# Adjacency of a graph network: indirect DMA scatters, or products of one-hot matrices copied to SBUF strips

## The chip, the cores and the metric

The kernel runs on one core of a Trainium2 chip. TensorE (PE) multiplies matrices and writes to PSUM, VectorE (DVE), ScalarE (ACT) and GpSimd (POOL) work on rows of 128 partitions, and SyncE (SP) issues most transfers. The metric is the device time of one execution in microseconds. The time of the kernel before is the median of ten runs.

## The reference

A graph of 3125 nodes with 128 features and 50,000 weighted edges goes through four layers, each followed by a residual sum and a layer norm. The edges come sorted by their destination.

```python
edge_index = jnp.stack([src, dst])
x = _layernorm(x + L0(x, edge_index, edge_weight, ...))   # three graph convolutions with relu
x = _layernorm(x + L1(x, edge_index, ...))                # attention over the edges
x = _layernorm(x + L2(x, edge_index, edge_attr, ...))     # gated messages of the edges
x = _layernorm(x + L3(x, edge_index, edge_weight, ...))   # ten graph convolutions with layer norm and gelu
```

A graph convolution of layers 0 and 3 is, with a loop of weight 1 added at every node:

```python
deg = segment_sum(w, dst); dinv = rsqrt(deg); norm = dinv[src] * w * dinv[dst]
out = segment_sum((x @ W)[src] * norm[:, None], dst) + b
```

## The kernel before

The nodes are padded to 3200 rows, 25 tiles of 128 (`x`, laid out partition by tile), and the edges to 50,176, 392 columns of 128. A convolution is a dense product: the adjacency matrix, 3200 sources by 3125 destinations in f32, lies in DRAM in seven banks of 464 destination columns (the last has 341). `Convolutions.sums` multiplies one bank with the scaled features, 25 tiles into one PSUM tile `acc`; each f32 product is two passes on PE, so two matmuls in the profile. A bank is read in five pieces of five tiles (`adj_k`, 1160 KB); some pieces stay in SBUF for all layers (seven in layer 0, ten in layer 3). `acc` goes to `aggT`, is multiplied by the weights into `po` (line 685), and `done` adds bias and activation and writes the next layer's features `xs`. That second half of a bank is put into the next bank's products, after the seventh.

The matrix is made with scatters. In the front, `fill` (line 115) writes zeros and the identity to all banks, seven issues on ACT's queue. `SortedBuild` reads the edges in six passes, each with its neighbourhood: `compare` adds up edges with the same source and destination and computes addresses (`adj_index`, line 126), `split` and `degrees` build one-hot matrices of the destinations, which PE adds up to the degrees in `deg_ps`; `dinv` is their inverse root (line 536). `stretches` checks that the edges are sorted and that the assumptions of this path hold; its flag chooses between this path and a general one (lines 1611 to 1627). DVE runs all of it in an order written out by hand (`InOrder`).

After the branch `SortedBuild.scatter` (line 538) issues one indirect DMA for each of 406 columns of 128 edges, on POOL's queue. A load of a bank waits for the scatters of its pass (`after`, line 555). Since the scatters come bank by bank, the first two layers are computed in pieces in an order that a table `AHEAD` (line 38) gives: whatever is loaded is used at once, with partial sums kept in `part`. The third layer runs plainly. Banks run from the seventh down to the first.

`Attention` (line 1007) prepares tables for layer 1. Its constructor runs in the front: transfers through DRAM (`dst_pad`, then `wide`), `fresh`, `dl` and four PE transposes to `s_local`. `tables` (line 1081) writes each finished bank of layer 0 to the tables that layer 1 gathers from with POOL. Layers 1 and 2 are `l1_sorted` and `l2_sorted`, and `l3` runs ten convolutions.

Of the kernel before, what the change touches and what calls it, by code (L numbers as in the profile page):

```python
# [23 lines left out]
BW = 464  # L24
CK = 5
LATE = 6
SC = 14


PASSES = ((20, 28, 5, 7, 5), (16, 21, 0, 5, 4), (12, 16, 0, 4, 3), (8, 12, 0, 3, 2), (3, 8, 0, 2, 1),  # L30
          (0, 3, 0, 1, 0))
BELOW = ((20, 5), (16, 4), (12, 3), (8, 2), (3, 1))
FROM = ((21, 5),)
HALF = 5
ALL = (0, 1, 2, 3, 4)


AHEAD = ((0, 6, ALL), (0, 5, ALL), (0, 4, ALL), (1, 6, (0, 1)), (1, 5, (0, 1)), (1, 4, (0, 1)),
         (0, 3, ALL), (1, 3, (0, 1)),
         (0, 2, ALL), (1, 2, (0, 1, 2)), (1, 6, (2,)), (1, 5, (2,)), (1, 4, (2,)), (1, 3, (2,)),  # L40
         (0, 1, ALL), (1, 1, (0, 1, 2, 3)), (1, 6, (3,)), (1, 5, (3,)), (1, 4, (3,)), (1, 3, (3,)), (1, 2, (3,)),
         (0, 0, ALL), (1, 0, (0, 1, 2, 3)), (1, 6, (4,)), (1, 5, (4,)), (1, 4, (4,)), (1, 3, (4,)), (1, 2, (4,)),
         (1, 1, (4,)), (1, 0, (4,)))
# [3 lines left out]
SPAN = SC + 2 * NEAR  # L47
HEADS, HD = 4, 32
# [10 lines left out]
def tile_gnn_stack(ctx: ExitStack, tc: tile.TileContext, a: dict, out: bass.AP):  # L59
# [33 lines left out]
    tables_adj = [(dram.tile([SPARE + (b1 - b0) * NP * BW, 1], F32, name=f"adj{b0}"), b0, b1)  # L93
                  for b0, b1 in ((0, HALF), (HALF, NBK))]

    def bank(b):

        table, b0, _ = tables_adj[b >= HALF]
        at = SPARE + (b - b0) * NP * BW
        return table[at:at + NP * BW, :].rearrange("(t p c) o -> p t (c o)", p=P, c=BW)  # L100

# [13 lines left out]
    def fill(pool, banks):  # L115
        wide = NP - P + NBK * BW
        eye = pool.tile([P, wide], F32, name="eye")
        nc.vector.memset(eye[:, :NP - P], 0.0)
        nc.gpsimd.memset(eye[:, NP:], 0.0)
        nc.gpsimd.tensor_copy(eye[:, NP - P:NP], ident)  # L120
        for b in banks:
            v = eye[:, b * BW:b * BW + BW]
            nc.scalar.dma_start(bank(b), bass.AP(tensor=v.tensor, offset=v.offset,
                                                 ap=[v.ap[0], [P, NT], [1, BW]]))

    def adj_index(ve, at, hi_i, step, src, dst, table, lo, hi, outer):

        b0 = tables_adj[table][1]
        ve.tensor_single_scalar(hi_i, src, P.bit_length() - 1, op=OP.logical_shift_right)
        ve.scalar_tensor_tensor(at, hi_i, -2.0 * P, src, op0=OP.mult, op1=OP.add)  # L130
        ve.scalar_tensor_tensor(at, at, float(BW), dst, op0=OP.mult, op1=OP.add)
        ve.tensor_scalar_add(at, at, float(SPARE + (NP - P) * BW - b0 * BW + (lo - b0) * BW * (NP - 1)))
        for b in range(lo + 1, hi):
            ve.tensor_scalar(step, dst, b * BW - 0.5, float(BW * (NP - 1)), op0=OP.is_gt, op1=OP.mult)
            ve.tensor_add(at, at, step)
        ve.tensor_single_scalar(outer, dst, lo * BW - 0.5, op=OP.is_lt)
        ve.tensor_single_scalar(step, dst, hi * BW - 0.5, op=OP.is_gt)
        ve.tensor_max(outer, outer, step)
# [100 lines left out]
    def stretches(ve, between):  # L239
# [5 lines left out]
        with (  # L245
# [5 lines left out]
            nc.sync.dma_start(first_i[:, 1:NS], bass.AP(  # L251
                tensor=dst.tensor, offset=dst.offset + SE, ap=[[0, 1], [SE, NS - 1]]))
            ones = one.tile([P, P], F32, name="ones")
            nc.vector.memset(ones, 1.0)
            spread = one.tile([P, NS + 1], F32, name="spread")
            nc.vector.memset(spread, 0.0)
            nc.vector.tensor_copy(spread[0:1], first_i)
            firsts = ps.tile([P, NS + 1], F32, name="firsts")
            nc.tensor.matmul(firsts, ones, spread, start=True, stop=True)
            nc.vector.tensor_copy(first_f, firsts)  # L260
            run = one.tile([P, NCH + NEAR], I32, name="run")
            nc.vector.memset(run[:, NCH:], NP)
            nc.sync.dma_start(run[:, :NCH], bass.AP(
                tensor=dst.tensor, offset=dst.offset, ap=[[NCH, P], [1, NCH]]))
            nc.sync.dma_start(run[:P - 1, NCH:], bass.AP(
                tensor=dst.tensor, offset=dst.offset + NCH, ap=[[NCH, P - 1], [1, NEAR]]))
            between()
            bad = one.tile([P, 3 + len(BELOW + FROM)], F32, name="bad")
            for i, (c, b) in enumerate(BELOW + FROM):
                ve.tensor_single_scalar(bad[:, 3 + i:4 + i], first_f[:, c:c + 1], b * BW - 0.5,  # L270
                                               op=OP.is_gt if i < len(BELOW) else OP.is_lt)
            scr = one.tile([P, NCH], F32, name="scr")
            ve.scalar_tensor_tensor(scr, run[:, :NCH], 0.0, run[:, 1:NCH + 1], op0=OP.add,
                                           op1=OP.is_gt, accum_out=bad[:, 0:1])
            ve.tensor_tensor(scr, run[:, :NCH], run[:, NEAR:], op=OP.is_equal)
            ve.scalar_tensor_tensor(scr, run[:, :NCH], float(N), scr, op0=OP.is_lt, op1=OP.mult,
                                           accum_out=bad[:, 2:3])
            ve.scalar_tensor_tensor(scr[:, :NS], first_f[:, 1:], 1.0 - P, first_f[:, :NS],
                                           op0=OP.add, op1=OP.is_gt, accum_out=bad[:, 1:2])
            total = ps.tile([P, 3 + len(BELOW + FROM)], F32, name="total")  # L280
# [8 lines left out]
    def build():  # L289
        with (  # L290
# [4 lines left out]
        ):  # L295
            blank = b1.tile([P, NCH], F32, name="blank")
# [9 lines left out]
            for i, (table, t0, t1) in enumerate(tables_adj):  # L306
                nc.sync.dma_start(table[:SPARE, :].rearrange("(p c) o -> p (c o)", p=P), blank)
                place = b1.tile([P, NCH], F32, name=f"place{i}")
                outer = b1.tile([P, NCH], F32, name=f"outer{i}")
                step = b1.tile([P, NCH], F32, name="step")  # L310
                hi_i = b1.tile([P, NCH], I32, name="hi_of_src")
                adj_index(nc.vector, place, hi_i, step, cols.src_i, cols.dst_f, i, t0, t1, outer)
                away = first_rows(b1, 0, place, NCH, f"away{i}")
                places.append((table, place, outer, away))
# [66 lines left out]
    class SortedBuild:  # L381
# [5 lines left out]
        def __init__(self, pool):  # L387
            self.at, self.total, self.ready, self.last = [], [], {}, []
            self.passes = list(enumerate(PASSES))
            self.st = [self.load(pool, 0, nc.sync)]  # L390

        def load(self, pool, q, queue):

            W = NEAR - 1
            s0, s1, lo, hi, _ = PASSES[q]
            C, e0 = SC * (s1 - s0), SE * s0

            def window(v, name, left, none):
                t = pool.tile([P, left + C + W], v.dtype, name=f"{name}{q}")
                n = left + C + W  # L400

                def part(p0, p1, c0, c1):
                    queue.dma_start(t[p0:p1, c0:c1], bass.AP(
                        tensor=v.tensor, offset=v.offset + e0 + p0 * C - left + c0,
                        ap=[[C, p1 - p0], [1, c1 - c0]]))

                first, last = e0 < left, e0 + P * C + W > NCH * P
                assert not (first and last) and W <= C
                if first:
                    nc.vector.memset(t[:, :left], none)  # L410
                    part(0, P, left, n)
                    part(1, P, 0, left)
                elif last:
                    nc.vector.memset(t[:, left + C:], none)
                    part(0, P, 0, left + C)
                    part(0, P - 1, left + C, n)
                else:
                    part(0, P, 0, n)
                return t

            return {"C": C, "e0": e0, "banks": (lo, hi), "src": window(a["src_r"], "src_w", W, -1),
                    "dst": window(a["dst_r"], "dst_w", W, 0), "ew": window(a["ew_r"], "ew_w", 0, 0.0)}

        def prepare(self, pool, scratch, ps, ve):

            W, st = NEAR - 1, self.st
            st += [self.load(scratch, q, nc.gpsimd) for q in range(1, len(PASSES))]
            pe_ = InOrder(nc.tensor)
            iota_ps = ps.tile([P, P], F32, name="iota_b")
            deg_ps = ps.tile([P, 3, NT], F32, name="deg_ps")  # L430
            CM = SC * max(s1 - s0 for s0, s1, _, _, _ in PASSES)

            def neighbours(t, start, C):

                v = t[:, start:start + C]
                return bass.AP(tensor=v.tensor, offset=v.offset, ap=[v.ap[0], [1, C], [1, W]])

            def compare(q):

                t = st[q]  # L440
# [37 lines left out]
                at = pool.tile([P, C], I32, name=f"at{q}")  # L478
                ve.tensor_add(at, away, place)
                self.total.append(total)  # L480
                self.at.append(at)

            def split(q):

# [1177 lines left out]
```

## Time and profile before

| | |
|---|---|
| median of 10 runs | 3357.58 us (3354.35 to 3362.06) |
| profiled execution, own time | 3359.69 us |
| its span | 3358.0 us |
| granted TensorE clock, mean | 0.935 |
| PE, DVE, ACT, POOL busy | 82%, 48%, 24%, 35% of the span |
| DMA | 627.98 MB, mean 187 GB/s |
| layer 0 with its front | 0 to 813 us |
| layer 1 | 813 to 1360 us |
| layer 2 | 1360 to 1960 us |
| layer 3 | 1960 to 3358 us |

The stages are read from the timeline: layer 1 begins with the first gather at 813.4, layers 2 and 3 with the reload of `x` that ends before them. The page's second part shows the span in forty slices of 84 us, each digit a busy share in tenths:

```profile
PE   0028557997888887578888869999999999999998
DVE  8991000222567667479999962322322322332234
ACT  0000000011111111467777721211111211111121
POOL 4777775002777774077777700000000000000000
PEclk9999778998688888789999979999999999999999
```

The first ten slices are layer 0 with its front. PE does nothing in the first two while DVE is full; POOL works for seven slices. In the last seventeen slices, layer 3, PE is full. A group line of the profile gives line, engine, operation, output and inputs, shape and count, then busy time and the mean duration of one, then the idle time of the engine just before and what ended it. DMA issues by a queue (SPq, ACTq) are not work of the engine.

### The profile page before, as it was taken

How to read it: one execution, taken by the hardware profiler on the slowest of the kernel's cores; microseconds unless marked ns; L12 is line 12 of the kernel's file. 1: busy time of each engine (PE TensorE's matmuls, PEld its weight loads, DVE VectorE, ACT ScalarE, POOL GpSimd, SP SyncE). 2: the span in 40 equal slices, each digit the busy share in tenths (PEclk: the TensorE clock that was granted, in tenths of full speed). 3: DMA queues.
4: the chain of work that ended last, by engine and by line, in shares of the span. 5: the costliest groups of instructions: out<-in, count | busy, mean ns of one | idle time of the engine just before them, and what ended most of it. 6: DMA issues, size and time to landing. Idle time of an engine off the chain costs nothing.

```text
span 3358.0 us, 33008 instructions
## 1 busy us (share of the span) xinstructions
PE 2743.3 (82%) x11351; PEld 1728.2 (51%) x11379; DVE 1615.2 (48%) x4421; ACT 797.0 (24%) x1236; POOL 1167.2 (35%) x1223
## 2 busy tenths in 40 slices
PE   0028557997888887578888869999999999999998
PEld 0024223554777776256666645555555555555554
DVE  8991000222567667479999962322322322332234
ACT  0000000011111111467777721211111211111121
POOL 4777775002777774077777700000000000000000
PEclk9999778998688888789999979999999999999999
DMA  9707247774344442566666686666676666666655
GB/s 344 218 1 239 85 153 244 244 255 133 94 103 103 104 104 72 148 205 200 206 198 200 185 275 228 200 224 211 195 234 207 204 224 205 216 207 217 220 193 184
DMA packets 443807, 627.98 MB, mean 187 GB/s; under 512 B 89721, under 2 KB 411406, under 8 KB 443614
## 3 DMA queue, kind: packets, MB, share of 16 engines
q1 hardware_dynamic: 361950, 498.10, 46.3%
q0 software_dynamic: 44960, 78.31, 8.8%
q10 hardware_dynamic: 36720, 49.38, 4.3%
q8 instruction: 91, 1.49, 0.2%
q14 instruction: 86, 0.70, 0.1%
HBM read 561.47 MB, written 64.38 MB: 186 GB/s over the span
## 4 chain that ended last, share of the span: by engine, by line
PE 50%; POOL 26%; issue 10%; DVE 6%; DMA 6%; ACT 2%; DVEq 0%; SPq 0%; POOLq 0%; ACTq 0%
PE acc L665 46%; POOL adj L545 10%; POOL xj L215 9%; POOL zj L215 6%; PE po L685 2%; DMA zj<-s_to_src,src_i 2%; PE sums L187 1%; DMA ew_w<-in_ew_r 1%; DVE z L187 1%; DVE msg L187 1%; DMA xj<-s_right,src_o 1%; DMA x<-s_after 1%; DVE pz L187 1%; DVE gate L187 1%; ACT parts L988 0%
## 5 line engine op out<-in xcount | busy, mean ns | idle before, releaser
L665 PE MATMUL acc<-adj_k,xs 128*128 128x464 f32 (+1 forms) x3340 | 1285.5, 539 | 0.0
L665 PEld LDWEIGHTS acc<-adj_k,xs 128*128 128x128 f32 x3340 | 629.9, 190 | 595.1 <-issue 556.5
L665 PE MATMUL acc<-adj,xs 128*128 128x464 f32 (+1 forms) x1210 | 479.1, 542 | 103.6 <-DMA adj<-adj 94.7
L215 POOL DMA_INDIRECT xj<-s_right,src_o x392 | 379.5, 968 | 362.7 <-issue 359.7
L215 POOL DMA_INDIRECT zj<-s_to_src,src_i x392 | 375.4, 958 | 237.9 <-DVE h L990 118.8
L545 POOL DMA_INDIRECT adj<-total,at x406 | 398.3, 981 | 153.5 <-issue 122.8
L665 PEld LDWEIGHTS acc<-adj,xs 128*128 128x128 f32 x1210 | 231.2, 194 | 313.4 <-issue 291.6
L699 DVE SCALAR_TENSOR_TENSOR v<-po,dinv,three 128x128 f32<-128x128 f32 x250 | 71.2, 345 | 589.2 <-PE po L685 589.2
L187 PE MATMUL pz<-w,eaT 128*128 128x256 f32 x784 | 244.7, 394 | 91.1 <-DVE msg L187 77.0
L187 PE MATMUL sums<-msg,of_edge 128*128 128x132 f32 (+1 forms) x1568 | 234.4, 318 | 15.2 <-DVE msg L187 15.2
L187 PEld LDWEIGHTS sums<-msg,of_edge 128*128 128x128 f32 x1568 | 227.4, 232 | 16.2 <-DVE msg L187 15.9
L187 PE MATMUL zT<-ident,xj 128*128 128x128 f32 x784 | 148.4, 317 | 77.3 <-DMA xj<-s_right,src_o 76.5
L711 ACT ACTIVATE rs<-rs 128x4 f32<-128x4 f32 (+1 forms) x91 | 18.6, 205 | 758.5 <-DVE rs L710 758.4
L187 PE MATMUL pz<-td,of_node 128*128 128x256 bf16 x1176 | 194.8, 275 | 0.5 <-DVE of_node L187 0.5
L187 PEld LDWEIGHTS zT<-ident,xj 128*128 128x128 f32 x784 | 126.5, 215 | 111.4 <-DMA xj<-s_right,src_o 96.8
L187 PEld LDWEIGHTS pz<-w,eaT 128*128 128x128 f32 x784 | 119.8, 193 | 115.6 <-DVE msg L187 96.9
L187 PE MATMUL deg_ps<-ohw,ohl 128*128 128x75 bf16 x406 | 30.3, 258 | 177.8 <-DVE ohw L187 177.8
L676 DVE COPY aggT<-acc 128x464 f32<-128x464 f32 x36 | 23.1, 642 | 314.3 <-PE acc L665 314.3
L678 ACT ACTIVATE aggT<-acc 128x464 f32<-128x464 f32 (+1 forms) x48 | 25.5, 532 | 603.9 <-PE acc L665 570.7
L187 ACT ACTIVATE leaky<-zT 128x512 f32<-128x512 f32 (+1 forms) x112 | 60.9, 544 | 373.6 <-PE zT L187 373.6
L187 PEld LDWEIGHTS <-of_node 128*128 128x128 bf16 x1176 | 116.0, 99 | 63.4 <-issue 1.4
L1556 ACT ACT_TABLE_LOAD x74 | 94.9, 1283 | 180.7 <-DVE v L1555 180.6
(202 smaller groups left out, 3026.8 us busy)
## 6 DMA issues: line engine op xcount, KB each, us to landing
adj_k<-adj SPq DMA_DIRECT2D x292, 1160.0 KB
adj<-eye ACTq DMA_DIRECT2D x7, 5800.0 KB
adj_k<-adj SPq DMA_DIRECT2D x42, 852.5 KB
adj<-adj SPq DMA_DIRECT2D x14, 1160.0 KB
eaT<-in_ea_t SPq DMA_DIRECT2D x56, 256.0 KB
drow<-s_local SPq DMA_DIRECT2D x28, 448.0 KB
eaT<-in_ea_t SPq DMA_DIRECT2D x56, 192.0 KB
drow<-s_local SPq DMA_DIRECT2D x56, 128.0 KB
```

Of the source, the lines that this page charges most:

```text
L187: ins = getattr(self.engine, name)(*args, **kwargs)
L215: after_writers(nc.gpsimd.indirect_dma_start(out=to, out_offset=None, in_=table[:NP, :], in_offset=bass.IndirectOffsetOnAxis(ap=index[:, c ...
L545: s = nc.gpsimd.indirect_dma_start(out=table[:SPARE + (hi - b0) * NP * BW, :], out_offset=bass.IndirectOffsetOnAxis(ap=self.at[q][:, c:c + ...
L665: nc.tensor.matmul(acc[:, :c1 - c0], xs[:, NT - 1 - j * CK - q, :], k[:, q, :c1 - c0], start=(n == 0), stop=(n == len(tiles) - 1))
L676: nc.vector.tensor_copy(to, acc[:, :c1 - c0])
L678: nc.scalar.activation(to, acc[:, :c1 - c0], AF.Copy)
L685: nc.tensor.matmul(po[:, t - t0, :], self.aggT[:, t * P:(t + 1) * P], w, start=True, stop=True)
L699: nc.vector.scalar_tensor_tensor(to[:, t - t0, :], sums[:, t - t0, :], dinv[:, t:t + 1], bias, op0=OP.mult, op1=OP.add)
L711: nc.scalar.activation(rs[:, :n], rs[:, :n], AF.Sqrt)
L1556: nc.scalar.activation(v, v, AF.Gelu)
```

## The change

The scatters, the fill, the comparisons and the table `AHEAD` go from the sorted path. The edges are laid out as 564 columns of 89 own edges (`OWN`), read as rows of 128 so that a destination's edges are complete in one column. `SortedEdges.prepare` computes for each edge its source's low part (0 to 127), a number `place` = 9 x (source's tile) + (destination's distance from the last destination of the column before), and its weight split into three bf16 parts; PE transposes them to edges on partitions. `degrees` adds the weights by destination within a column and sends the sums through 45 one-hot products. For each chunk of 14 columns `matrices` builds, on DVE, one-hot matrices of `place` and of the low part, the latter times each of the three weights. For each column PE multiplies them, three bf16 products into a PSUM tile of 128 x 225: source's low part by (tile, destination within the window of 9). ACT copies it to the bank's strip in SBUF at a column offset from a register, one copy per bank that the column touches. When a strip is whole, POOL adds the identity, SP stores it to DRAM, and the first convolution's products of that bank are issued from the strip, one at every other column, beginning six columns later.

```diff
+        def matrices(self, pool, c0, n):
...
+            ve.tensor_tensor(place[:, :n].rearrange("p c (a b) -> p c a b", b=2),
+                             self.pairs.rearrange("p (a b) -> p a b", b=2)[:, None].to_broadcast([P, n, h, 2]),
+                             v[:, :, None, :].to_broadcast([P, n, h, 2]), op=OP.is_equal)
...
+            ve.tensor_tensor(low, self.lows.rearrange("p (a b) -> p a b", b=2)[:, None].to_broadcast([P, n, P // 2, 2]),
+                             self.low[:, c0:c0 + n, None, :].to_broadcast([P, n, P // 2, 2]), op=OP.is_equal)
...
+            for i in range(3):
+                ve.tensor_tensor(heavy[:, i, :n].rearrange("p c (a b) -> p c a b", b=2), low,
+                                 self.parts[:, i, c0:c0 + n, None, :].to_broadcast([P, n, P // 2, 2]), op=OP.mult)
+            return place, heavy
+
+        def offsets(self, b, c0, c1):
...
+            return nc.values_load_multi_w_load_instructions(
+                self.at[0:1, at:at + c1 - c0], engines=(mybir.EngineType.Activation,), min_val=0,
+                max_val=MARGIN + BW, skip_runtime_bounds_check_because="bounded above")[1]
+
+        def build(self, strips, pool, ps, adj, use):
...
+            def whole(b):
...
+                    nc.gpsimd.tensor_add(v, v, ident[:, d0 - t * P:d1 - t * P])
+                k = strip[b][:, :, MARGIN:MARGIN + c1 - c0]
+                nc.sync.dma_start(adj.bank(b)[:, :, :c1 - c0], k)
+                steps.append(use(b, k))
...
+            for g, (c0, n) in enumerate(chunks):
+                if g + 1 < len(chunks):
+                    hot[g + 1] = self.matrices(pool, *chunks[g + 1])
+                place, heavy = hot.pop(g)
+                at = {b: (max(c0, FIRST[b]), self.offsets(b, max(c0, FIRST[b]), min(c0 + n, UPTO[b])))
+                      for b in range(NBK) if max(c0, FIRST[b]) < min(c0 + n, UPTO[b])}
+                for c in range(c0, c0 + n):
+                    if c % 2 == 0:
+                        two = ps.tile([P, 512], F32, name="side", bufs=3)
+                    to = two[:, c % 2 * 256:c % 2 * 256 + NT * WIN]
+                    for i in range(3):
+                        lanes.tensor.matmul(to, heavy[:, i, c - c0, :], place[:, c - c0, :NT * WIN],
+                                            start=(i == 0), stop=(i == 2))
+                    for b, (first, places) in at.items():
+                        if FIRST[b] <= c < UPTO[b]:
+                            if b not in strip:
+                                strip[b] = strips.tile([P, NT, MARGIN + BW + WIN], F32, name="strip")
+                            lanes.scalar.activation(strip[b][:, :, bass.ds(places[c - first], WIN)],
+                                                    to.rearrange("p (t d) -> p t d", d=WIN), AF.Copy)
+                    for b in range(NBK):
+                        if c == UPTO[b] - 1:
+                            whole(b)
+                            wait = 6
+                    if wait:
+                        wait -= 1
+                    elif c % 2:
+                        go_on()
```

There are two strips and two sets of `of_pair` and `heavy`. A bank's columns are taken by bounds that hold for any edges that the flag admits (`FIRST`, `UPTO`), so that neighbouring banks share 11 to 16 columns, 81 in all. During the build the order on PE, DVE and ACT is fixed (`lanes.pin()`), and `x` itself, scaled by POOL, is the first layer's features:

```diff
+    def l0_sorted(edges, adj, attention):
...
+            for b in range(NB):
+                t0, t1 = tiles4(b)
+                nc.gpsimd.tensor_mul(x[:, t0:t1, :], x[:, t0:t1, :], dinv_rows(t0, t1))
...
+                lanes.pin()
+                edges.build(strips, hot, ps, adj, lambda b, strip: conv.sums(x, b, *layers[0], strip))
+                lanes.free()
...
+                load_nodes()
+                conv.xs[0] = hold.tile([P, NT, D], F32, name="xs0")
+                conv.pieces(stream, hold, 6, InOrder(nc.sync))
+                attention.prepare(hold, ps, nc.vector)
+                for i in (1, 2):
+                    conv(conv.xs[i % 2], *layers[i])
+                conv.finish()
+                conv.end()
```

Behind the build `x` is loaded again, the work of `Attention`'s constructor that needs scratch (now `prepare`) follows, and layers two and three of layer 0 read their pieces from DRAM with six held. Banks run from the first up, tiles too. Layer 3 holds nine pieces in place of ten, since the tiles of `SortedEdges` stay allocated. The front's tiles are loaded on all three queues, and `x` is loaded at its very start. The general path keeps its scatters, with the fill moved into it; it does not run with these edges.

## The prediction

> **What bounds the kernel now.** I read the windows by stage first: layers 0 (three graph convolutions, to 813 us), 1 (813 to 1360), 2 (to 1960) and 3 (to the end). The diff only touches what comes before 813, and which pieces layer 3 holds.
>
> ```profile
> 0.00:255.00 255.00, 31.54 (x410) 28.99 (x410) 236.92 (x346) 1.51 (x2) 171.53 (x196) 1.00 0.57 185
> 255.00:524.00 269.00, 161.07 (x439) 83.85 (x440) 22.27 (x48) 3.14 (x6) 205.91 (x208) 0.83 0.47 155
> 524.00:652.00 128.00, 128.00 (x378) 67.63 (x379) 22.11 (x51) 1.11 (x2) 34.87 (x36) 0.98 0.80 270
> 652.00:813.00 161.00, 150.80 (x465) 82.10 (x463) 43.93 (x159) 27.40 (x75) 0.00 (x0) 0.96 0.63 211
> ```
>
> The columns after the length are the busy times of PE, PEld, DVE, ACT and POOL, then the granted clock, the DMA share and GB/s. Until 255 DVE works alone (key comparisons, degrees); until 524 POOL's scatters hold PE, which is busy for 161 of 269 us at a clock of 0.83; from 524 PE is full, with 270 GB/s beside it. The chain of waits says what ends the second stage, and the groups what it consists of:
>
> ```profile
> 515.39 2.14 DMA adj<-total,at
> 517.79 5.90 DMA adj<-adj
> 523.83 25.84 PE acc L665 x60
> ```
>
> ```profile
> L545 POOL DMA_INDIRECT adj<-total,at x406 | 398.3, 981 | 153.5 <-issue 122.8
> L187 PE MATMUL pz<-td,of_node 128*128 128x256 bf16 x1176 | 194.8, 275 | 0.5 <-DVE of_node L187 0.5
> ```
>
> So 406 scatters at 1.27 us (busy and issue) end at about 568, and layer 0 follows them. The first gather of layer 1 starts at 813.4 in the timeline: this is the time to beat. What the change must keep below it is front, build, layers two and three of the convolution.
>
> **Front.** Removed: the fill (seven issues of 5800 KB), the neighbour comparisons, 29 groups of degree matrices at 3.65 us. The new front is a chain on DVE. Its first data I put at 14 us (the first ew_w came at 13.3, behind the fill; 8 to 20). Checks: five operations of 392 to 565 elements at about 0.57 and small ones with two PE products, 5 us. Preparation: nine of 640 elements at 0.4 to 0.75 (392 take 0.57, 1050 take 1.25), 6 us; PSUM to SBUF 1128 wide, three at 1.25 and two halves at 0.66, 5; fourteen offsets at 0.19, 2.7; PE, 1. Degrees: 15 operations of 1152 elements at 0.7 to 1.3, 16.5; one-hot rows (5760 and four of 1170 elements) 8; 45 products at 0.075 (14 take 1.05 now), 3.4; the tail 2 as now; branch 2.6 (the flag is there at 45.5, the first scatter goes at 48.1). Sum: 66 us, where dinv came at 254.8. Range 58 to 80.
>
> **Build and first convolution.** 564 columns of 89 edges each; per column three bf16 products 128x225 on PE, one or (81 times) two copies by ACT to a strip, with a register address; per chunk of 14 columns five DVE operations and one register load per bank (53 loads of up to 14 registers, 645 in all). Per engine:
>
> PE: three 128x256 bf16 products take 0.325 us with new weights each in the dense timeline of layer 2 (start to start), so 0.1 for 225 columns: 0.3 per column. A convolution product of two f32 passes costs 0.78 (25 in 19.46). They are put at every other column, from six columns after a strip is whole: 25 pairs of columns at 6 x 0.1 + 0.78 = 1.38, 34.5 us for about 52 columns. The other 32 of a bank's 84 columns are ACT's.
>
> ACT: 128x128 from PSUM takes 0.26, 128x256 0.38, 128x464 0.56, so 225 elements 0.36. Each copy waits for the one before it (the strips overlap), as exp and ln do in layer 2 (1.04 long, 1.07 apart); with the address instruction partly behind it I take 0.42. Bounds: 0.29 (independent 128x256 copies start 0.29 apart) and 0.55 (0.36 and the address instruction's 0.18, below). No row shows a load of many registers. The nearest are SP's:
>
> ```profile
> 1016.67 0.34 SPq L187 DMA_DIRECT2D s_after<-y  x1
> 1017.60 0.34 SPq L187 DMA_DIRECT2D hl<-s_left  x1
> ...
> 1005.69 0.37 SPq L187 DMA_DIRECT2D s_logits<-e  x1
> 1006.24 0.37 SPq L187 DMA_DIRECT2D xw<-s_before  x1
> ```
>
> Between the first two lie a load of one register and an address instruction, 0.59; between the last two an address instruction alone, 0.18: so 0.4 for one register. Fourteen cost between 0.4 and 14 x 0.4 = 5.7 us. As it is one instruction I stay near the lower end: 1.0. [...]
>
> So the 32 columns hold about 45 copies (19 us) and 3.3 loads (3.3): 22.5. At each strip's end POOL adds the identity in four or five pieces (its 128x128 copy takes 0.28) before PE may start: 3 us not covered by the six columns; bounds are nothing, and 5 x (0.28 + 1.1, a DVE operation ahead of each piece) = 7. [...] The trace has scatters at 0.99 us beside a DVE that is 97% busy (80 to 252), but no POOL arithmetic there.
>
> DVE: per chunk 3164 + 4 x 1792 = 10,332 elements of bf16. One-source bf16 takes 0.32 ns each (2660 in 0.85), f32 operands 1.12 (1792 in 2.02): between 3.3 and 11.6 us. Two sources read twice what one does, so I take 0.6: 6.2 us, 37 per bank of six chunks, with 2.4 of results. It lies behind the 60 us below; if that cover is gone, DVE sets 72 to 74 per bank.
>
> A bank is then 34.5 + 22.5 + 3 = 60. First strip, with no convolution beside it: 6 for the first chunk, 100 copies 42, 7 loads 7, 3: 58. Five more strips 300, the short last one 36, its 3, and its own convolution 16 (15.77 now). Build: 413 us. DVE's and ACT's evictions of acc are in PE's shadow. The stores of the strips (5.8 MB each 60 us, 97 GB/s) have what the fill had.
>
> **Behind the build.** x is reloaded after PE's last read, then SP issues seven small writes, order and the first adj piece; wide waits for the padded dst, and the other adj loads queue behind it. PE has four transposes of dl, which wait for order, ahead of layer two. Moved from the front, this all stands open: x 0.9, small ones 3, order 0.4, landing 5.9 as adj above, dl and transposes 2, PE's restart 2: 14 us (8 to 25). Layer two: 136.7 in layer 3 (20 us per bank), here with all 35 pieces, 39 MB, x and wide 3 more, 305 GB/s wanted; 317 was reached for 20 us and 270 over 128, so 142 (137 to 156). Layer three with its tables 144, as 652.4 to 796.3 now, and the tail to the first gather 17 (796.3 to 813.4).
>
> Sum: 66 + 413 + 14 + 142 + 144 + 17 = 796, 17.4 before 813.4. Layer 3 holds nine pieces for ten: 26 loads per 136.7 us, 220 GB/s for 212, and PE waits for no DMA there now: nothing. It also runs the banks upwards, which only moves the short bank from the first place to the last. Layers 1 and 2 keep their order. The profiled execution took 3359.7 (span 3358.0); less 17.4 and its 2.1 over the median of the runs, 3340.
>
> **Rivals.**
> (a) The register loads bind, on the slow side. Place: ACT, at each chunk in the 32 columns that PE leaves to it. Price: 0.4 + 14 x 0.18 (an address instruction per register) = 2.9 us. About 28 of the 53 loads stand open, so 1.9 x 28 = 53 us more: 3393. For it: nothing else is between ACT's copies; against it: it is one instruction. It decides from 1.0 + 17.4 / 28 = 1.6 us per load. At 5.7 ACT alone needs 645 x 0.42 + 302 = 573, and the time is near 3520.
> (b) DVE stays at one element per cycle: 72 per bank and some 490 in all, 3417. For it: operands repeated from two-element rows, which no row of now has; against: bf16 one-source is four times as fast.
> (c) ACT overlaps: copies 0.30, loads 0.4. The 32 columns shrink to 15 us and the first strip to 42: 356 in all, 3283. For it the 0.29 between independent copies, against it the wait for the copy before.
> (d) The flag sends the kernel to the other branch: the edges' longest window spans 7 nodes of the 9 allowed, so no.
>
> **How the numbers follow.** Forecast 0.45 (own range 3310 to 3365: front, gap, layer two and hand-over at their bounds, seldom all at one end), (a) 0.23, (b) 0.10, (c) 0.21, (d) 0.01. A measurement tells 0.2%, 7 us. In the forecast's case 0.75 of the chance is faster, 0.1 the same; with (c), faster 0.55, same 0.05, slower 0.40. From 3285 to 3415 leaves out the far ends of (a), half of (c) and half of (b).
>
> **What would show it.** dinv at 66 and no PE wait in the dense columns; POOL empty from 100 to 796; strips 60 us apart; a bf16 of_low at 1.1 us, not 2; copies 0.42 apart, and a gap of about 1 us on ACT before each chunk; first gather at 796. Wrong if ACT's gaps at the chunks exceed 1.6, if of_low takes 2, or if layer two's PE waits for adj_k.

## The result

The changed kernel takes 3662.77 us (median of 8 runs, 3658.67 to 3667.85), the kernel before 3357.77 beside it: a ratio of 1.091 (95% interval 1.09 to 1.0919), slower by 305 us. The profiled execution has a span of 3662.8 us.

By stages, in the view of windows (span, then busy times of PE, PEld, DVE, ACT and POOL, granted clock, DMA share, GB/s), the changed kernel:

```profile
64.00:785.00 721.00, 420.98 (x2031) 255.01 (x2032) 253.55 (x238) 230.90 (x648) 21.48 (x37) 0.83 0.14 51
785.00:810.00 25.00, 15.71 (x63) 10.48 (x61) 3.75 (x13) 0.46 (x1) 0.59 (x2) 0.86 0.83 254
810.00:950.00 140.00, 133.37 (x376) 68.69 (x377) 17.09 (x37) 1.67 (x3) 0.00 (x0) 0.96 0.89 300
950.00:1096.00 146.00, 146.00 (x452) 79.57 (x451) 34.52 (x127) 18.99 (x55) 0.00 (x0) 1.00 0.77 251
```

The stage from 64 to 785 is the build with the first convolution, and nothing in it is full: PE 421 of 721 us, DVE 254, ACT 231, and the memory moves 51 GB/s. Behind it layers two and three of layer 0 are full, and the first gather of layer 1 comes at 1121.0 where it came at 813.4. From there to the end it is 2541.8 us (before: 2544.6). So all of the loss lies before the first gather, and in one stage:

| step | forecast, us | measured, us |
|---|---|---|
| front, to the end of `dinv` | 66 | 64.5 |
| build and first convolution | 413 | 735 (64.5 to 799.6) |
| gap behind the build | 14 | 16.5 (to 816.1) |
| layers two and three, tail, to the first gather | 303 | 305 (to 1121.0) |

With no engine full (PE 421 of 721 us), this stage is a chain that hands over. The groups of instructions (busy time and mean ns, then the idle time just before them and what ended it):

```profile
L189 PE MATMUL side<-of_pair,heavy 128*128 128x225 bf16 x1692 | 306.6, 319 | 301.1 <-ACT strip L189 289.1 <-DVE heavy L189 12.0
L189 ACT ACTIVATE strip<-side 128x225 f32 x645 | 229.9, 371 | 489.4 <-PE side L189 351.0 <-issue 134.2 <-ACT strip L189 3.8
L189 PE MATMUL acc<-strip,x 128*128 128x464 f32 (+1 forms) x350 | 174.8, 595 | 0.0
```

PE waits 289 us for ACT's copies, and ACT 351 us for PE's products: each for the other, although `side` has three buffers. Another 134 us of ACT end with "issue", which is no wait for anything on record; the register loads below fill it. The convolution's own products never wait. The timeline at a dense stretch, PE and ACT with what ended the idle time before each line:

```profile
305.35 0.45 PE L189 MATMUL side<-of_pair,heavy 128*128 128x225 bf16 x3 [0.52 <-ACT strip L189]
305.64 0.96 PE L189 MATMUL acc<-strip,x 128*128 128x464 f32 x2
305.89 0.37 ACT L189 ACTIVATE strip<-side 128x225 f32 x1 [0.60 <-PE side L189]
306.43 0.45 PE L189 MATMUL side<-of_pair,heavy 128*128 128x225 bf16 x3
306.98 0.37 ACT L189 ACTIVATE strip<-side 128x225 f32 x1 [0.71 <-PE side L189]
307.40 0.45 PE L189 MATMUL side<-of_pair,heavy 128*128 128x225 bf16 x3 [0.52 <-ACT strip L189]
307.69 0.96 PE L189 MATMUL acc<-strip,x 128*128 128x464 f32 x2
```

This is one pair of columns, 305.35 to 307.40: 2.05 us where 1.38 was forecast. Read it down: the product of a pair's second column starts 0.05 us behind the copy of its first (306.98 + 0.37 and 307.40). The two columns are halves of one tile (`two`), and the product into the second half waits for ACT's copy of the first (0.52, the first line). In order on PE stands the convolution's product, then the next pair's first column; ACT then copies that column, and only this copy lets PE go on. Three tiles do not help: PE cannot run ahead past a wait (0.52 us here) that sits inside each of them.

The chain of waits at a chunk's border (start, length, what; ACTq is ACT's instruction queue, L583 the register load):

```profile
292.07 0.37 ACT strip L189
292.44 8.90 ACTq L583
301.34 0.06 issue
301.40 0.04 ACTq L189
301.44 0.04 issue
301.48 0.02 ACTq L189
301.50 0.04 issue
301.54 0.38 ACT strip L189
301.92 0.04 issue
301.97 0.72 PE side L189 x3
```

Here ACT loads registers for 8.90 us, and PE starts again behind the first copy after it. Of the 53 loads 51 stand on this chain, with 133 us together: most loads of 14 registers with 2.65 us, but five of them, in five different banks, with 8.8 to 9.2. What else runs beside the long one, by the DMA view of 292 to 301.5:

```profile
DMA packets 1809, 3.34 MB, mean 351 GB/s; under 512 B 15, under 2 KB 1808, under 8 KB 1808
q1 hardware_dynamic: 1808, 3.33, 94.0%
```

That is the finished strip's store, issued at 284.18. So there are two suspects: the tile that two columns share (theory H), and the register loads (theory L, the forecast's rival (a)).

### The profile page after: what moved, and what is told of

The parts are those of the page before. It is cut to its first block, busy times and chain, and to the rows that moved or that the text cites. A ratio compares the mean times of both kernels' runs of the same rounds, so it can differ in the third digit from the quotient of the medians.

```text
span 3662.8 us, 37114 instructions
## 1 busy us (share of the span) xinstructions
PE 3008.1 (82%) x12697; PEld 1895.3 (52%) x12725; DVE 1651.4 (45%) x4356; ACT 1028.7 (28%) x1884; POOL 777.5 (21%) x839
## 4 chain that ended last, share of the span: by engine, by line
PE 58%; POOL 11%; DVE 9%; issue 7%; DMA 5%; ACT 5%; ACTq 4%; SPq 0%; DVEq 0%; another core or an unknown queue 0%; POOLq 0%
PE acc L751 42%; POOL xj L217 7%; PE side L189 7%; POOL zj L217 5%; ACT strip L189 4%; ACTq L583 4%; PE acc L189 4%; PE sums L189 2%; PE po L766 2%; DMA zj<-s_to_src,src_i 2%; DMA xj<-s_right,src_o 1%; DVE z L189 1%; DVE msg L189 1%; DVE pz L189 1%; DVE gate L189 1%
## 5 line engine op out<-in xcount | busy, mean ns | idle before, releaser
L751 PE MATMUL acc<-adj_k,xs 128*128 128x464 f32 (+1 forms) x3180 | 1212.0, 536 | 1.7 <-DMA adj_k<-bank 1.7
L751 PEld LDWEIGHTS acc<-adj_k,xs 128*128 128x128 f32 x3180 | 598.8, 190 | 557.9 <-issue 509.4
L189 PE MATMUL side<-of_pair,heavy 128*128 128x225 bf16 x1692 | 306.6, 319 | 301.1 <-ACT strip L189 289.1
L189 PEld LDWEIGHTS <-heavy 128*128 128x128 bf16 x1692 | 199.6, 118 | 463.7 <-issue 437.1
L751 PE MATMUL acc<-adj,xs 128*128 128x464 f32 (+1 forms) x1020 | 405.5, 544 | 2.3 <-DMA adj<-bank 2.3
L189 ACT ACTIVATE strip<-side 128x225 f32 x645 | 229.9, 371 | 489.4 <-PE side L189 351.0
L751 PEld LDWEIGHTS acc<-adj,xs 128*128 128x128 f32 x1020 | 192.9, 191 | 187.4 <-issue 177.6
L189 DVE TENSOR_TENSOR of_pair<-pairs,place 128x3164 bf16<-128x3164 bf16 (+1 forms) x41 | 73.5, 1792 | 366.0 <-PE side L189 366.0
L793 ACT ACTIVATE rs<-rs 128x4 f32<-128x4 f32 (+1 forms) x91 | 18.7, 205 | 780.6 <-DVE rs L792 780.6
L189 PE MATMUL acc<-strip,x 128*128 128x464 f32 (+1 forms) x350 | 174.8, 595 | 0.0
L599 POOL TENSOR_TENSOR strip<-strip,ident 128x128 f32<-128x128 f32 (+8 forms) x31 | 10.7, 379 | 699.0 <-issue 589.8
```

Source lines behind the costliest of these rows:

```text
L189: ins = getattr(self.engine, name)(*args, **kwargs)
L599: nc.gpsimd.tensor_add(v, v, ident[:, d0 - t * P:d1 - t * P])
L751: lanes.tensor.matmul(acc[:, :c1 - c0], xs[:, t, :], k[:, q, :c1 - c0], start=(t == 0), stop=(t == NT - 1))
L793: nc.scalar.activation(rs[:, :n], rs[:, :n], AF.Sqrt)
```

## Experiments

The experiments ran on chips 2, 4 and 15, where the kernel before takes 4152 to 4188 us and the changed one 4130 to 4154; for the first profiles no chip is on record. The last section shows where the two sorts of runs part; the build of the changed kernel is the same to 5 us in both. So experiments are compared by the start of the first gather, which is 1121.0 in the first profile of the changed kernel, 1120.4 (`c0_changed`) and 1115.9 (`f2_changed`) in two more.

| run | what differs from the changed kernel | last product of the first convolution | first gather | time, us |
|---|---|---|---|---|
| `c0_changed`, `f2_changed` | nothing | 798.4, 794.0 | 1120.4, 1115.9 | 4152.9, 4137.9 |
| `e1_own_tile` | a PSUM tile per column | 564.6 | 886.5 | 3916.1 |
| `e2_fixed_at` | constant addresses, no loads (the strips are filled at wrong places) | 648.4 | 970.5 | 4005.2 |
| `e3_both` | e1 and e2 (wrong places too) | 417.6 | 739.6 | 3785.2 |
| `e4_seven` | loads of seven registers | 751.9 | 1074.0 | 4112.2 |
| `e5_spread` | e1, convolution at 2 of 5 columns | 567.3 | 889.3 | 3916.5 |
| `e6_parts` | e1, stores in four parts | 508.7 | 830.7 | 3858.3 |
| `e7_all` | e1, e4, e5, e6 | 529.2 | 851.0 | 3874.2 |
| `e8_packed`, `f1_packed` | e6, two addresses per register | 459.9, 458.0 | 782.2, 779.9 | 3807.5, 3807.0 |
| `e9_pairs` | both products before the two copies | 548.1 | 870.4 | 3892.1 |
| `e10_three` | e9, parts, packed addresses | 466.7 | 788.7 | 3807.3 |

**The two suspects, each alone and together.** Own tiles (`e1_own_tile`, and in `e3_both`):

```diff
-                    if c % 2 == 0:
-                        two = ps.tile([P, 512], F32, name="side", bufs=3)
-                    to = two[:, c % 2 * 256:c % 2 * 256 + NT * WIN]
+                    two = ps.tile([P, 512], F32, name="side", bufs=3)
+                    to = two[:, :NT * WIN]
```

> Each column's product gets a PSUM tile of its own (three tiles, one column each) in place of two columns sharing one. Nothing else changes. Theory H (shared tile): the product of a pair's second column waits for the copy of the first because they share a tile; each pair then costs 2.05 us beside the convolution and 1.81 us without it, in series on PE and ACT. With own tiles a pair costs what the busier engine needs: 1.38 on PE beside the convolution, about 1.14 on ACT (two copies 0.57 apart) otherwise. About 165 pairs x 0.67 + 112 pairs x 0.67 = 185 us less, near 3475. Rival L (the register loads alone set the loss, the wait between product and copy would be hidden without them): the same loads stand in the way, 3640 to 3670.

Constant addresses (`e2_fixed_at`, and in `e3_both`):

```diff
-                at = {b: (max(c0, FIRST[b]), self.offsets(b, max(c0, FIRST[b]), min(c0 + n, UPTO[b])))
+                at = {b: (max(c0, FIRST[b]), [((c - FIRST[b]) * 6) % (MARGIN + BW)
+                                              for c in range(max(c0, FIRST[b]), min(c0 + n, UPTO[b]))])
...
-                            lanes.scalar.activation(strip[b][:, :, bass.ds(places[c - first], WIN)],
+                            lanes.scalar.activation(strip[b][:, :, places[c - first]:places[c - first] + WIN],
```

> The copies go to constant addresses (six elements on per column, round the strip) and no register is loaded; two columns still share a PSUM tile. The strips then hold the columns at wrong places, so the convolutions' sums are not the reference's; every product, copy, store and convolution is still there. Theory L (loads): ACT's gaps of 2.65 to 8.9 us at the chunks vanish, 53 loads, about 130 us of the chain: near 3530. Theory H: the same 130 us, since in series with everything; the period of a pair stays 2.05 and 1.81 us. Rival F (the gaps are not the loads but code loading or the strip's store): the gaps stay, 3640 to 3670.

> Own PSUM tile per column and constant addresses together (the strips are again filled at wrong places). H and L together: 3663 - 185 - 130 = 3348, about the time before. If ACT's copies then follow each other at 0.57 us, ACT sets the stretches without convolution (about 45 copies per bank, 26 us) and PE the others (1.38 per pair, 35 us); if PE's slow products (0.215 us each in the first strip) are due to its idling, they fall to about 0.1 here. If only one of the two holds, 3475 or 3530.

Against 1121.0, own tiles bring the first gather forward by 234.5 us, constant addresses by 150.5, both by 381.4. The two gains add, to within 3.6 us (385.0). Theory H holds, with more than the 185 expected; where the other 50 come from is not shown. L holds as well, with more than 130. The rival that the gaps are something other than the loads is out. One thing besides the loads changes in `e2_fixed_at` and `e3_both`: without a register's address the copies follow each other faster (0.32 us apart in `e3_both`, 0.41 in `e8_packed`). The totals asked for in the expectations (3475, 3530, 3348) can't be read from these chips' times. With own tiles, PE in a dense stretch of `e1_own_tile` (timeline):

```profile
300.81 0.75 PE L189 MATMUL side<-of_pair,heavy 128*128 128x225 bf16 x6
301.39 0.96 PE L189 MATMUL acc<-strip,x 128*128 128x464 f32 x2
302.19 0.74 PE L189 MATMUL side<-of_pair,heavy 128*128 128x225 bf16 x6
302.77 0.96 PE L189 MATMUL acc<-strip,x 128*128 128x464 f32 x2
```

301.39 to 302.77 is 1.38 us per pair, and no wait in it: the forecast's dense columns, to the hundredth. Without loads but with the shared tile (`e2_fixed_at`, a stretch with no convolution) the wait is still there, once per pair:

```profile
300.11 0.74 PE L189 MATMUL side<-of_pair,heavy 128*128 128x225 bf16 x6 [0.52 <-ACT strip L189]
301.48 0.74 PE L189 MATMUL side<-of_pair,heavy 128*128 128x225 bf16 x6 [0.63 <-ACT strip L189]
302.86 0.74 PE L189 MATMUL side<-of_pair,heavy 128*128 128x225 bf16 x6 [0.63 <-ACT strip L189]
```

**Is it the tile, or the bank of PSUM?** `e9_pairs` keeps the shared tile and changes the order alone:

```diff
+                    made.append((c, to))
+                    if c % 2 or c + 1 in UPTO:
+                        for k, to in made:
...
+                                    lanes.scalar.activation(strip[b][:, :, bass.ds(places[k - first], WIN)],
+                                                            to.rearrange("p (t d) -> p t d", d=WIN), AF.Copy)
+                        made = []
```

> The changed kernel with two columns per PSUM tile as it is, but with both products of a pair issued before its two copies. Loads and stores as in the changed kernel. Theory H (the wait comes from product, copy, product, copy within one tile): PE no longer waits inside a pair and runs up to three pairs ahead, so the gain of the own tiles (1121 to 886.5) comes without any other tile, and more: six columns of lead cover most of a 2.65 us load: first gather between 840 and 890. Rival (sharing a PSUM bank itself makes PE and ACT wait for each other): 1080 to 1125.

The first gather is at 870.4, 250.6 us earlier with the same tiles, so it is not the sharing itself that costs them, but the order product, copy, product, copy within one tile. A lead of six columns for three is worth 16 us beside own tiles (886.5), so most of each load still stood open.

**What a load's time goes by.** `e4_seven` splits each load of 14 into two:

```diff
+                        m = min(f + CH // 2, u)
+                        at[b] = (f, [*self.offsets(b, f, m), *(self.offsets(b, m, u) if m < u else [])])
```

> Each register load is split into two of at most seven registers (about 95 loads for 53), with shared PSUM tiles as in the changed kernel. If a load's time goes by registers (14 x 0.19 = 2.65 us): 3655 to 3675, each load near 1.3. If it goes by load, whatever its size: about 42 more loads x 2.65 = 111 us more, near 3775.

Neither: 97 loads for 53 and the first gather 47 us earlier (1074.0). The loads of both kernels in the view of one line (minimum, median and maximum ns), first `e4_seven`, then the changed kernel:

```profile
L583 ACTq TENSOR_LOAD <-at x97: 285/1542/5964, 67.2 to 732.3; - x97
```

```profile
L583 ACTq TENSOR_LOAD <-at x53: 549/3010/9511, 67.2 to 779.7; - x53
```

Half the registers take half the time (1542 for 3010 ns), so the cost of these loads goes by register, about 0.22 us in this view (3010 / 14, 1542 / 7). The loads did not become less work: the gain lies in ACT's time that ends with "issue", 67.0 us for 134.2. So about half of the loads' time is now hidden behind ACT's waits for PE; this reading is argued, not tested.

**The long loads.** `e6_parts`, with own tiles, cuts each strip's store in four and issues a part behind the second copy of each following chunk:

```diff
-                nc.sync.dma_start(adj.bank(b)[:, :, :c1 - c0], k)
+                stores.extend((adj.bank(b)[:, t:min(t + 7, NT), :c1 - c0], k[:, t:min(t + 7, NT), :]) for t in range(0, NT, 7))
...
+                    if c == c0 + 1 and stores:
+                        tc.add_manual_dep(nc.sync.dma_start(*stores.pop(0)).ins, copy.ins.name, SYNC,
+                                          reason="behind the loads")
```

> Own PSUM tile per column, and each strip's store to DRAM (5800 KB, 15 us at 375 GB/s) is cut in four, one issued behind the second copy of each of the next four chunks, so that no register load falls into a store. Theory S (a load's registers are read one by one, and each read is slowed by the store: 0.19 us per register without, 0.8 with it): the six loads of 11.4 to 11.6 us fall to 2.65, 54 us less, first gather near 832. Rival C (these loads are long for another reason, such as code loading at the end of a bank): 880 to 892.

The loads of `e1_own_tile` and of `e6_parts`, same view:

```profile
L583 ACTq TENSOR_LOAD <-at x53: 547/2996/11976, 66.6 to 546.6; - x53
```

```profile
L583 ACTq TENSOR_LOAD <-at x53: 550/2996/3046, 67.5 to 490.7; - x53
```

The longest load falls from 11.98 to 3.05 us and the median stays: 830.7 for 886.5, 55.8 us for the 54 expected. It is shown that the store beside them made five loads (11.4 to 11.6 us on the chain of `e1_own_tile`) more than four times as long; that each register's read is slowed, as theory S has it, is not shown apart. The expectation had six such loads. Five by 8.8 us are 44, and the other 12 us are not traced.

**Spreading the convolution** over more columns (`elif c * 2 % 5 < 2` for `elif c % 2`), so that PE's work lies beside all of ACT's:

> Own PSUM tile per column, and the convolution's products at two of five columns in place of one of two, so that they spread over 62 columns of a bank and not 50. By the theory that, with own tiles, ACT (645 copies at 0.41 and the loads' 150 us, 415 in all) is now the longer engine and the dense stretch wasted its time beside PE: the build is ACT's 415 with 12 ahead and 23 behind, first gather near 840 where own tiles alone gave 886. Rival: ACT's waits for PE are only shuffled, 875 to 895.

889.3: the rival was right. ACT's waits for PE fell (135.9 to 103.7 us), but its time that ends with "issue", the stops at the loads, rose (110.5 to 141.2). Together with half loads and parts:

> Own PSUM tile, products at two of five columns, stores in four parts, and loads of at most seven registers (which took 47 us off the changed kernel). If these gains add: ACT has 264 of copies and 645 registers x 0.19 = 123 us, part of it behind PE's work: first gather between 770 and 815, so at or below the 813 of before. Rival: with half loads, the second one falls into a store's part and stays long; near 835.

851.0, worse than parts alone (830.7) and later than both forecasts, the rival's 835 the nearer. Its mechanism is in the trace: the second half load of a chunk now meets a store's part (ACT's stops at the loads are 0.9 to 1.4 us where none runs and mostly 2.9 to 3.5 where one does). `e5_spread` gave nothing to add.

**Fewer registers.** `e8_packed` packs two addresses into a register, with own tiles and parts:

```diff
+                ve.scalar_tensor_tensor(self.at[:, n:n + m], of[:, :, 1], 512.0, of[:, :, 0], op0=OP.mult, op1=OP.add)
...
+            return [nc.s_assert_within(v >> 9 if c % 2 else v & 511, 0, MARGIN + BW,
+                                       skip_runtime_bounds_check_because="bounded above")
...
```

> Own PSUM tile and stores in four parts, and two addresses packed into one register (a + 512 b), so that half as many registers are loaded (about 325 for 645, seven for 14 columns); each pair of copies costs an additional register operation. If the loads cost 0.19 us per register and ACT sets the pace: 60 us less than with parts alone (830.7), part of it already hidden: first gather between 770 and 790. Rival: the register operations cost what the loads save, 820 to 835.

> Both products of a pair before its copies, stores in four parts, packed addresses. ACT's work is then 645 copies at 0.41 = 264 us and 325 x 0.19 = 62 us of loads, PE's about 311; with six columns of lead most loads lie behind PE's work. Build between 352 (no loads at all) and 400: first gather between 745 and 785, which is 30 to 70 us ahead of the 813.4 of the kernel before. Rival: the loads still stand in the way as with own tiles, 785 to 815.

782.2 and 788.7: the register operation shows no cost between the copies (four take 1.59 us here and in `e6_parts`), and in the second the rival (785 to 815) was right and the theory (745 to 785) wrong: with the stops this short, six columns of lead bring no more than three. The timeline of ACT in `e8_packed` shows what is left, a stop of 1.44 us at a chunk's border:

```profile
204.06 0.78 ACT L189 ACTIVATE strip<-side 128x225 f32 x2 [0.52 <-PE side L189]
206.28 1.59 ACT L189 ACTIVATE strip<-side 128x225 f32 x4 [1.44 <-PE side L189]
208.34 0.78 ACT L189 ACTIVATE strip<-side 128x225 f32 x2 [0.47 <-PE side L189]
```

Four copies take 1.59 us, so they follow each other at (1.59 - 0.37) / 3 = 0.41, the forecast's 0.42. In `e3_both`, with constant addresses, the same reckoning gives 0.32 (30 copies in 9.57 us, from 252.82).

**Beside the kernel before.** The kernel before and two kernels again:

> The changed kernel as it is, for the runs sent with it. First gather of layer 1 near 1121 us, as in its first profile. The chip of the first four experiments gave 4165 us for the kernel before; where the gathers of layers 1 and 2 are slower, everything behind the first gather is longer for every kernel, so the time of the first gather is compared.

> The kernel before, profiled on the chip of these runs. Where it takes 4160 us in place of 3358, the question is which stages are longer: if layers 1 and 2 alone, then 490 us of the difference lie there, as in the changed kernel (4153 for 3663), and some 320 us more in the scatter stage and layer 0; the build of the changed kernel was the same to 1 us on both chips.

> The kernel with own PSUM tiles, stores in parts and packed addresses once more, with three rounds beside the kernel before. Its first gather was at 782.2 us, 31 us before the 813.4 of the kernel before on the chip of the first profiles and 357 before the 1139.1 on the chip of the last runs. If a kernel's time follows its first gather on either chip: 0.990 of the kernel before where that takes 3358 us (3326), 0.914 where it takes 4165 (3807). If the loss behind the gathers depends on when they start, neither.

> The changed kernel beside it. First gather at 1120 to 1122 us on any chip; 1.091 of the kernel before where that takes 3358 us, 0.996 where it takes 4165, since there the scatters of the kernel before hold DVE (gaps of up to 35 us) and its first gather comes at 1139 us in place of 813.

The changed kernel is at 0.9962 (0.9945 to 0.9978) and 0.9953 (0.9936 to 0.9971) of the kernel before on these chips, `e8_packed` at 0.9146 (0.9117 to 0.9175) and 0.9156 (0.9123 to 0.9188). The kernel before has its first gather at 1139.1 here, 18.7 us behind the changed kernel's 1120.4 and 356.9 behind `e8_packed`; the times differ by 15 (4167.8 and 4152.9) and 360 us. So time follows the first gather here. Where the kernel before takes 3358 us `e8_packed` was not run; if time follows there too, it is 31.2 us ahead of the kernel before (813.4), an estimated 3327 us.

## Why the prediction was wrong

**The step that failed** is "25 pairs of columns at 6 x 0.1 + 0.78 = 1.38" with "no PE wait in the dense columns", and with it the copies at 0.42 in the other 32. Products and copies have these durations (1.38 per pair in `e1_own_tile`, 0.41 per copy in `e8_packed`). But both lines assume that PE runs ahead of ACT, by three tiles. The diff says otherwise: two columns write halves of one tile, and a product, a copy, a product and a copy of it follow in this order. A pair then costs 2.05 for 1.38 beside the convolution. Without it, it costs 1.81 in the first strip, and 1.37 in the later stretch of `e2_fixed_at` above, for two copies at 0.42; six products take 1.29 us in the one and 0.74 in the other, and the last section has the granted clocks beside them. Undoing it alone gives back 234.5 us.

**The register load** was the right mechanism with the wrong size: 1.0 us against 2.65, near the 2.9 of rival (a). Rival (a) came out at 3393 because it let 25 of 53 loads lie in PE's shadow. With PE stopped inside each pair there is no shadow, so nearly all of them counted: 133 us on the chain, 150.5 by constant addresses, against 27 in the forecast (7 in the first strip, 3.3 in each of the other six). About a fifth of that was on nobody's list: the five long loads beside the stores, 5 x 6.3 = 31 us (55.8 in `e6_parts`, beside loads that take 11.4 to 11.6 with own tiles). The forecast had costed the stores by their bytes (97 GB/s, harmless), not by what they do to a load.

**The rest of the build** was overestimated. Without both, `e3_both` needs 353 us from `dinv` to the last product (64.5 to 417.6), against 413 - 27 = 386. These 33 us have two candidates, which the runs do not part. One is the forecast's 3 us per bank for the identity, 21 in all: the convolution's products waited 0.0 us. The other is that the copies of `e3_both`, without a register's address, follow each other at 0.32 for the forecast's 0.42. That 353 + 234.5 + 150.5 = 738 comes near the measured 735 says no more than that the two gains add.

**Right:** the front (64.5 for 66), `of_low` at 1.1 us (1.9 only in the first chunk, while POOL scaled `x`) and so rival (b) out, layers two and three (305 for 303), layer 3's nine pieces at no cost, the branch. The gap behind the build (16.5 for 14) is near by luck: on its chain of waits the reload of `x` stands with 8.2 us, for 0.9 in the forecast's sum, and the small writes, 3 in that sum, lie behind it. Rival (c) put its number, 3283, on copies that overlap and loads that cost little; `e3_both`, which has copies at 0.32 and no loads, reaches 739.6, 73.8 us ahead of the kernel before's 813.4, so it was near the price of a kernel that this one was not.

## What to carry to other kernels

Count how far a producer can run ahead in the order of instructions, not in buffers: a tile that is written, read, written and read again in parts was one buffer with a handover inside here, though there were three such tiles (own tiles gave back 234.5 us, `e1_own_tile`). A stage in which no engine is full wants the two groups that wait for each other; here the sum of their steps was the period, not the larger one (2.05 us per pair for PE's 1.38). And where addresses come from registers, price the load by register (here 2.65 us for 14, 0.19 each), count all that stand in series with the engine that uses them, and keep large transfers away from them (8.8 to 9.2 us for 2.65 beside a strip's store).

## What was not expected of the hardware

**Register loads slow down beside a transfer.** 14 registers take about 2.65 us on the chain of waits of the changed kernel, and 8.8 to 9.2 beside a strip's store (359 to 394 GB/s in the DMA view of 292 to 301.5, until the store ends); in `e1_own_tile` 11.4 to 11.6. `at`, from which they are read, lies in SBUF.

**Between short waits PE's granted clock fell from 1.00 to 0.50.** In the first strip, with no convolution between the products, six of them take (timeline of the changed kernel):

```profile
78.45 1.29 PE L189 MATMUL side<-of_pair,heavy 128*128 128x225 bf16 x6 [0.52 <-ACT strip L189]
```

These are 0.215 us each. In `e1_own_tile` six take 0.58 from start to the next instruction (300.81 to 301.39), 0.097 each. The trace of the changed kernel has no clock record before 182 us, and its view of windows then shows 1.00, whatever the products take. The trace of `e2_fixed_at` begins its clock records at 63 us, and its first strip has the same six products in 1.29. Its view of windows, with the granted clock ahead of the DMA share:

```profile
100.00:150.00 50.00, 35.45 (x166) 23.64 (x166) 23.88 (x20) 20.73 (x57) 2.04 (x3) 0.50 0.00 0
290.00:306.00 16.00, 10.87 (x69) 6.95 (x68) 6.45 (x6) 6.70 (x18) 0.45 (x1) 1.00 0.00 1
312.00:326.00 14.00, 9.03 (x42) 6.01 (x42) 6.00 (x6) 7.71 (x27) 0.96 (x1) 0.50 0.00 1
```

Between the last two a bank's convolution products end (the last starts at 298.35), and the timeline shows the fall:

```profile
306.98 0.74 PE L189 MATMUL side<-of_pair,heavy 128*128 128x225 bf16 x6 [0.63 <-ACT strip L189]
308.35 1.22 PE L189 MATMUL side<-of_pair,heavy 128*128 128x225 bf16 x6 [0.63 <-ACT strip L189]
310.09 1.29 PE L189 MATMUL side<-of_pair,heavy 128*128 128x225 bf16 x6 [0.52 <-ACT strip L189]
```

So where PE had only these products, with a wait of 0.52 to 0.63 us in each pair, six came to take 1.29 us for 0.74, beside a clock of 0.50 for 1.00. Between 284 and 330 us of `e2_fixed_at` no wait of PE's products for ACT is longer than 0.8 us, so no long stop came before the fall. That the waits brought it about is the author's reading, not shown alone, and the runs do not part its price from the 234.5 us.

**Two sorts of runs.** In the runs of the experiments DVE and ACT wait beside POOL's indirect DMAs, for something that the profile calls `remote` because it can't tell the releaser. The view of waits over the whole span (total, times, longest), first the kernel before there (`c1_before`), then the changed kernel there (`c0_changed`):

```profile
DVE ohl L187 <- remote: 321.8, 10, 35.5
ACT leaky L187 <- remote: 264.1, 20, 52.7
DVE z L187 <- remote: 185.7, 30, 36.5
```

```profile
ACT leaky L189 <- remote: 302.9, 20, 52.0
DVE z L189 <- remote: 213.7, 34, 33.7
```

`leaky` and `z` belong to layers 1 and 2, whose gathers both kernels have. `ohl` is a degree matrix of the kernel before, which lies beside its scatters: its last one starts at 676.2 there, at 248.4 in the first profile, and the first gather comes at 1139.1 for 813.4. The first profiles have no such line in either kernel. POOL's median scatter takes the same 0.97 us in both. The cause stays open, the chip included: that the scatters hold DVE, as `f2_changed` expected, is not shown. But when the first gather comes in the kernel before (813.4 and 1139.1), and with it the verdict on this change, differs between the two sorts: a ratio of 1.091 in the first, 0.995 to 0.996 in the others, which is under 2% and counts as the same.
